# End of attention: an earlier division for the last group, rows scaled and written behind both halves' scores, one queue for the first half's scores

## The chip, the cores and the metric

The kernel runs on one core of one Trainium2 chip. The metric is the device time of the program in microseconds (us): the median of its runs. Engines are named as the profile names them: PE (matrix products and transposes), DVE (vector), ACT (activation), POOL (general), SP (issues transfers only).

## The reference, cut to what matters

The input `x` has 8 batches of 1024 tokens with 256 features. One layer of attention with 16 heads of 16 features, then a layer in which each of 8 experts picks the 1024 tokens that score highest for it:

```python
x = x + attention(layernorm(x), Wq, Wkv, Wout, bout)
xf = layernorm(x).reshape(-1, 256)              # 8192 rows
scores = softmax(xf @ gate_w.T, axis=-1)        # 8 experts
vals, idx = top_k(scores.T, 1024)               # each expert takes 1024 rows
y = layernorm(xf[idx]) * ln_w + ln_b
out = gelu(y @ fc1s + b1s) @ fc2s + b2s
xf = xf.at[idx].add(out * vals)                 # scattered back
x = x + xf
```

No expert can start before the scores of all 8192 tokens are known, since its threshold is found over all of them.

## The kernel before, in words

**Attention in steps.** The work is cut into 32 groups (8 batches, 4 groups of 4 heads each), and a group into 16 steps: two halves of 512 queries, 8 blocks of 128 keys in each. The loop counts steps `s` over all groups, from -13 to 512. In a step `step_pair` (twice) issues the score products (L581) and their exponentials on ACT (L614), and for a later group, 13 steps ahead, the products and maxima of L530 and L537. In every even step `weigh_values` multiplies the exponentials of the two steps before with the values (16 passes, L633), copies the result from PSUM with ACT (L642, L646) and adds it up on POOL (L648); the last sum of the last group's second half goes to DVE. At step 512 only the last `weigh_values` is left.

**Tasks between the steps.** What isn't part of that pattern is written as generators. `Task.advance` runs a generator up to its next `yield`: a number means "not for so many steps", a letter says what kind of piece comes next. `run_pieces` is called at the end of each step and advances each task in `urgent` once, and the first one in `ends`. When the last keys of a half were weighed, `weigh_values` puts `divide` (L652) in `urgent`. It waits 4 steps, becomes a piece of kind "y", and in the following step transposes the sums (L659), inverts the denominators (L665) and scales (L667). Once the last group of a batch has a half divided, the half's `epilogue` (L699) enters `ends`. Its pieces are, in order: nothing; the transposes of the attention output (L251, called from `transposed`) and their copies (L712); the output product of two token blocks and the residual sum (L719, L727); the same for the other two blocks; the statistics of one block (L219, L220), four times, the last followed by the scale (POOL, L222 and L224), the normalised rows `xf` (L242), the second layer norm's scale `rs_c` (POOL, L232 to L236), the sum `x + xf` (POOL, L733) and, in the last batch, the write of `out` (L734); transposes of `xf` (L251, L761); the gate product and its copy `lg` (L767, L775); transposition, maximum, difference and exponential (L778 to L786); the softmax's division into `sc` (L789 to L793); the transposition of the scores (L798), their copy `turned` (L800), four transfers of them into `by_expert` (L803), and in the last batch the scaled rows (L744, four, from `xf` and `rs_c` into `rows`) and their write to memory (L808).

**After the loop** `finish(urgent)` drives what is left of the divisions to the end at once, and the two epilogues of the last batch are advanced in turn, first half, second half, first half and so on, with no regard to the waits. When step 512 is over, the first half's epilogue has done its pieces up to the first output product, and the second half's hasn't begun.

**Order and buffers.** Each engine runs its instructions in the order of the text; a wait on one holds up all behind it on that engine. Inside attention this order is kept as written; the experts' part has a block of its own. `lg` and `turned` of both halves share one buffer (`tag="lg"`, `bufs=1`). In the last batch the first half's four transfers into `by_expert` are shared out between SP and ACT (L803: `last and t % 2`), as are the second half's.

**Search and experts.** DVE finds the threshold of all experts at once in 30 rounds over `by_expert` (L1003, with PE's L1007, then L1009 and L1012), makes the token lists, and POOL gathers rows from `rows_d` (L1146). The first weights are loaded by SP (L953, L955) behind the transfers of attention.

Of the kernel before, what the change touches and what calls it, by code (L numbers as in the profile page):

```python
# [19 lines left out]
P = 128  # L20
# [7 lines left out]
def preln_attention_moe_kernel(  # L28
# [18 lines left out]
    nc = tc.nc  # L47
    B, N, D = x.shape
    E = gate_t.shape[1]
    FF = fc1_t.shape[2]  # L50
    T = N // P
# [6 lines left out]
    NG = H // 4  # L58
# [5 lines left out]
    rows_d = dram.tile([B * N, ROW], F32, name="rows_d")  # L64
# [33 lines left out]
    with ExitStack() as actx:  # L98
# [10 lines left out]
        T2 = T // 2  # L109
# [514 lines left out]
        def weigh_values(i, half, chunk):  # L624

            b, g = divmod(i, NG)
            pa = ps_m.tile([P, QW], F32, tag="m", name="ps_av")
            for n, (kt, es) in enumerate(chunk):  # L630
                for h in range(4):
                    c = VS * (4 * g + h)
                    nc.tensor.matmul(  # L633
                        pa[HS * h : HS * (h + 1), :],
                        lhsT=v_bufs[b % 2][:, kt, c : c + HS],
                        rhs=es[h // 2][:, h % 2, :],
                        start=(n == 0),
                        stop=(n == len(chunk) - 1),
                    )
            if chunk[0][0] == 0:  # L640
                grp[i]["av"] = small.tile([P, QW], F32, tag="av", name="av")
                nc.scalar.copy(grp[i]["av"], pa)  # L642
            else:
                av = grp[i]["av"]
                part = small.tile([P, QW], F32, tag="avp", name="avp", bufs=3)
                nc.scalar.copy(part, pa)  # L646
                end = i == B * NG - 1 and half == 1 and chunk[-1][0] == T - 1
                (nc.vector if end else nc.gpsimd).tensor_tensor(av, av, part, ALU.add)  # L648
                if chunk[-1][0] == T - 1:
                    urgent.append(Task(divide(i, half, av)))  # L650

        def divide(i, half, av):  # L652

            b, g = divmod(i, NG)
            yield 4
            yield "y"
            pt = ps_m.tile([P, T2, 4, HS], F32, tag="m", name="ps_d")
            for t in range(T2):
                nc.tensor.transpose(  # L659
                    pt[:, t].rearrange("p h d -> p (h d)"), av[:, t * P : (t + 1) * P], ident  # L660
                )
            if b not in outs:
                outs[b] = side.tile([P, T, D], F32, tag="ao", name=f"ao_{b}")
            rden = small.tile([P, T2, 4, 1], F32, tag="rden", name="rden")
            nc.vector.reciprocal(rden, pt[:, :, :, DH : DH + 1])  # L665
            dst = outs[b][:, T2 * half : T2 * (half + 1), 4 * g * DH : 4 * (g + 1) * DH]
            nc.vector.tensor_tensor(  # L667
                dst.rearrange("p t (h d) -> p t h d", h=4),
                pt[:, :, :, 0:DH],
                rden.to_broadcast([P, T2, 4, DH]),  # L670
                ALU.mult,
            )
            finished[(i, half)] = True
# [17 lines left out]
        def add_bias(xt):  # L691
            nc.gpsimd.tensor_tensor(xt, xt, bo.unsqueeze(1).to_broadcast([P, T2, D]), ALU.add)

        def residual_ahead(b, hf):
            xt = residual(b, hf)
            yield 5
            add_bias(xt)

        def epilogue(b, hf):  # L699
            ao = outs[b]  # L700
            tok = slice(hf * QW, (hf + 1) * QW)
            last = b == B - 1
# [5 lines left out]
            own = last and hf == 1  # L708
# [4 lines left out]
            for t2 in range(T2 // 2):  # L713
                yield "x"
                po = ps_m.tile([P, 2, D], F32, tag="m", name="ps_o")
                for j in range(2):
                    t = 2 * t2 + j
# [16 lines left out]
            out_dma = lambda: nc.sync.dma_start(  # L734
                out[b, tok, :].rearrange("(t p) d -> p t d", p=P), xt
            )
            if last:
                out_dma()

            rows = side.tile([P, T2, ROW], F32, tag="rows", name=f"rows_{b}_{hf}")  # L740

            def rows_scaled():
                for t in range(T2):
                    eng.tensor_scalar(  # L744
                        rows[:, t, 0:D], xf[:, t, :], rstd2[:, t : t + 1], None, ALU.mult
                    )
# [53 lines left out]
            nc.scalar.copy(turned, ps[0 : T2 * E, 0:P])  # L800
            t0 = b * T + hf * T2
            for t in range(T2):
                (nc.scalar if last and t % 2 else nc.sync).dma_start(  # L803
                    by_expert[t0 // T2 :: NB, t * P : (t + 1) * P], turned[t * E : (t + 1) * E, :]
                )
            if last:
                rows_scaled()
            nc.sync.dma_start(  # L808
                rows_d[t0 * P : (t0 + T2) * P, :].rearrange("(t p) d -> p t d", p=P), rows
            )  # L810

# [56 lines left out]
        for s in range(-LEAD, n_steps + 1):  # L870
            i, step = divmod(s, 2 * T)
            b, g = divmod(i, NG)
            half, kt = divmod(step, T)
# [17 lines left out]
            if with_exp or with_max:  # L891
                es = []
                for pair in range(2):
                    es.append(
                        step_pair(
                            pair,
                            (mi, mstep) if with_max else None,
                            (i, half, kt) if with_exp else None,
                        )
                    )  # L900
                if with_exp:
                    if s % 2 == 0 and before:
                        weigh_values(*before[0][:2], [c[2] for c in before])
                        before = []
                    before.append((i, half, (kt, es)))
            elif before:
                weigh_values(*before[0][:2], [c[2] for c in before])
# [13 lines left out]
            for hf in range(2):  # L921

                if s >= 0 and b < B and finished.pop((NG * b + NG - 1, hf), None):
                    ends.append(Task(epilogue(b, hf), batch=b))
                if b > 0 and finished.pop((NG * b - 1, hf), None):
                    ends.append(Task(epilogue(b - 1, hf), batch=b - 1))
        finish(urgent)
        for hf in range(2):
            if finished.pop((NG * B - 1, hf), None):
                ends.append(Task(epilogue(B - 1, hf)))  # L930
# [488 lines left out]
```

## Time and profile before

| what | value |
|---|---|
| three runs | 2234.91, 2235.82, 2239.15 us; median 2235.82 |
| profiled execution | 2235.39 us, of which the span of instructions is 2233.4 |
| mean granted clock of PE | 0.968 |
| last exponential of attention (L614) ends | 1665.95 us |
| last 16 passes of L633 | 1665.01 to 1667.05 us |
| first half's `xf` (L242), second half's | 1678.79 us, 1686.22 us |
| first half's `turned`, second half's (L800) | 1691.26 us, 1696.34 us |
| first round of the search (L1003) | 1699.83 us |
| first gather (L1146) | 1761.31 us |

All times in the table and in what follows count from the first instruction of the span. The profile was taken of one execution; its page gives busy time by engine, 40 slices of the span, the chain of work that ended last, and groups of like instructions. The timeline lists single instructions with what ended the idle time ahead of them ("[2.17 <-DMA by_expert<-turned]"). The view of stretches gives, for each stretch from A to B, its length, the busy time of PE, PE's weight loads, DVE, ACT and POOL with the number of instructions, then PE's granted clock, the DMA engines' busy share and GB/s.

### The profile page before, as it was taken

The page shows a single profiled execution, that of the slowest core. Times are in us where ns is not written, and L with a number is a line of the kernel's source. Part 1 is how long each engine was busy: PE and PEld are TensorE (multiplying, and loading weights), DVE is VectorE, ACT ScalarE, POOL GpSimd, SP SyncE. Part 2 cuts the span into 40 slices and gives each one's busy share as a digit, 9 for nine tenths or more (in the row PEclk, how much of TensorE's full clock was granted, in tenths as well). Part 3 has the DMA queues.
Part 4 walks back from the last instruction along what each step waited for, and adds up shares of the span by engine and source line. Part 5 has one row for each costly group of instructions (what it writes and reads, how often), then busy time and mean ns, then how long its engine had stood idle before and what let it go on. Part 6 is the DMA issues. An engine that isn't in the chain of part 4 may idle for free.

```text
span 2233.4 us, 35022 instructions
## 1 busy us (share of the span) xinstructions
PE 2065.1 (92%) x12476; PEld 1098.2 (49%) x12476; DVE 1816.9 (81%) x3444; ACT 1382.3 (62%) x1782; POOL 1294.7 (58%) x1319
## 2 busy tenths in 40 slices
PE   7999899999999999999999999999982499999998
PEld 4444444444444444444444444444441266666665
DVE  7988788988898899889989988989936657777754
ACT  2677777877787877878778877877770012222222
POOL 6657666748585856758584766734142154555542
PEclk7999999999999999999999999999995699999999
DMA  6413723632362256236324722652113033333322
GB/s 182 168 59 129 268 75 130 228 135 78 134 238 87 89 205 212 90 111 234 130 77 154 269 73 79 218 174 85 41 39 134 20 74 72 76 76 75 70 48 25
DMA packets 152702, 271.51 MB, mean 122 GB/s; under 512 B 15056, under 2 KB 67664, under 8 KB 152400
## 3 DMA queue, kind: packets, MB, share of 16 engines
q1 hardware_dynamic: 139056, 250.61, 32.7%
q0 software_dynamic: 12288, 17.05, 4.6%
q8 instruction: 98, 1.61, 0.3%
q10 hardware_dynamic: 1184, 1.62, 0.2%
q14 instruction: 76, 0.62, 0.1%
HBM read 143.93 MB, written 125.04 MB: 120 GB/s over the span
## 4 chain that ended last, share of the span: by engine, by line
PE 70%; DVE 19%; issue 5%; DMA 2%; ACT 2%; POOL 1%; SPq 0%; POOLq 0%; ACTq 0%; DVEq 0%
PE ps_av L633 21%; DVE mx L537 14%; PE ps_x L530 13%; PE ps L1224 8%; PE ps_o L1278 7%; PE ps_s L581 7%; PE ps_p L288 6%; PE ps_t L251 3%; PE ps_o L719 3%; PE ps_h L1183 1%; ACT e L614 1%; DVE low L1123 1%; PE ps_d L659 1%; DMA top_d<-mrows 1%; DVE xr L727 1%
## 5 line engine op out<-in xcount | busy, mean ns | idle before, releaser
L537 DVE TENSOR_REDUCE mx<-ps_x 128x1 f32<-128x512 f32 x2048 | 1265.3, 682 | 162.5 <-PE ps_x L530 149.4
L614 ACT ACTIVATE e<-ps_s 128x1024 f32<-128x1024 f32 x1024 | 995.7, 1025 | 89.2 <-PE ps_x L530 39.9
L530 PE MATMUL ps_x<-k,q 64*128 64x512 f32 x2048 | 720.8, 452 | 19.7 <-DVE mx L537 7.0
L581 PE MATMUL ps_s<-q,s 64*128 64x512 f32 x2048 | 624.3, 429 | 9.2 <-ACT e L614 6.0
L530 PEld LDWEIGHTS ps_x<-k,q 64*128 64x128 f32 x2048 | 348.5, 186 | 416.5 <-DVE mx L537 286.3
L633 PE MATMUL ps_av<-e,v 128*32 128x512 f32 x4096 | 495.9, 602 | 7.4 <-DVE mx L537 1.3
L648 POOL TENSOR_TENSOR av<-av,avp 128x512 f32<-128x512 f32 x191 | 243.7, 1276 | 404.7 <-ACT avp L646 383.4
L581 PEld LDWEIGHTS ps_s<-q,s 64*128 64x128 f32 x2048 | 314.6, 185 | 47.8 <-ACT e L614 30.3
L1288 POOL DMA_INDIRECT out<-o,idx x64 | 114.9, 1796 | 216.1 <-DVE o L1287 80.5
L1278 PE MATMUL ps_o<-w,hT 128*128 128x256 f32 x1024 | 230.2, 381 | 0.0
L633 PEld LDWEIGHTS ps_av<-e,v 128*32 128x32 f32 x4096 | 107.6, 109 | 244.5 <-issue 165.8
L1278 PEld LDWEIGHTS ps_o<-w,hT 128*128 128x128 f32 x1024 | 191.8, 190 | 29.3 <-issue 4.8
L646 ACT COPY avp<-ps_av 128x512 f32<-128x512 f32 x192 | 112.7, 587 | 148.5 <-PE ps_av L633 145.9
L1236 ACT COPY mid<-ps 128x512 f32<-128x512 f32 x28 | 16.0, 571 | 203.7 <-PE ps L1224 203.7
L288 PE MATMUL ps_p<-wqkv,xnT 128*128 128x512 f32 (+1 forms) x288 | 134.5, 596 | 6.0 <-DVE mx L537 5.3
L1176 ACT ACTIVATE hT<-mid,b 128x512 f32<-128x512 f32 x112 | 77.9, 718 | 98.9 <-DVE mid L1251 73.9
L269 POOL TENSOR_TENSOR u<-pe,sin 128x256 f32<-128x256 f32 (+1 forms) x128 | 86.2, 696 | 56.5 <-ACT pe L263 56.5
L1146 POOL DMA_INDIRECT g<-rows_d,idx x64 | 70.0, 1094 | 83.5 <-issue 75.2
L1286 DVE TENSOR_TENSOR o<-ps_o,b2b 128x256 f32<-128x256 f32 x64 | 27.0, 422 | 103.2 <-PE ps_o L1278 93.7
L335 POOL CAST hi<-full 128x512 fp32r<-128x512 f32 x60 | 36.8, 614 | 90.3 <-ACT full L333 83.7
L273 POOL TENSOR_TENSOR qk<-pe,u 128x512 f32<-128x512 f32 (+1 forms) x72 | 83.3, 1157 | 7.6 <-DVE pe L271 2.6
L336 POOL TENSOR_TENSOR lo<-full,hi 128x512 fp32r<-128x512 f32 x60 | 77.0, 1283 | 6.7 <-DMA s_d<-dlo 2.1
(194 smaller groups left out, 2368.9 us busy)
## 6 DMA issues: line engine op xcount, KB each, us to landing
s<-s_d SPq DMA_DIRECT2D x64, 512.0 KB
k<-k_d SPq DMA_DIRECT2D x62, 512.0 KB
q<-q_d SPq DMA_DIRECT2D x124, 256.0 KB
s_d<-dhi SPq DMA_DIRECT2D x32, 512.0 KB
s_d<-dlo SPq DMA_DIRECT2D x32, 512.0 KB
w<-in_fc_t SPq DMA_DIRECT2D x16, 1024.0 KB
q_d<-hi SPq DMA_DIRECT2D x30, 512.0 KB
q_d<-lo SPq DMA_DIRECT2D x30, 512.0 KB
```

Source lines behind the costliest of these rows:

```text
L269: eng.tensor_tensor(u[:, :, a * hd : (a + 1) * hd], v4[:, :, 1 - a, :], s3, ALU.mult)
L288: nc.tensor.matmul(pp, lhsT=xnT[:, kc, t % T2 * P : (t % T2 + 1) * P], rhs=w.rearrange("p a d -> p (a d)") if n == DC else w, start=(kc == 0),
L530: nc.tensor.matmul(pt, lhsT=q[r : r + 64, h // 2, j * P : (j + 1) * P], rhs=k[r : r + 64, h // 2, kh * QW : (kh + 1) * QW], start=True, st ...
L537: nc.vector.tensor_reduce(grp[i]["mx"][:, kh, h, j : j + 1], pt, AX.X, ALU.max)
L581: nc.tensor.matmul(pt[:, h % 2, :], lhsT=ones_r[r : r + 64, :] if last else k[r : r + 64, pair, kt * P : (kt + 1) * P], rhs=(top_bufs[half ...
L614: nc.scalar.activation(e.rearrange("p h q -> p (h q)"), pt.rearrange("p h q -> p (h q)"), AF.Exp, scale=DH**-0.5,)
L633: nc.tensor.matmul(pa[HS * h : HS * (h + 1), :], lhsT=v_bufs[b % 2][:, kt, c : c + HS], rhs=es[h // 2][:, h % 2, :], start=(n == 0), stop= ...
L646: nc.scalar.copy(part, pa)
L648: (nc.vector if end else nc.gpsimd).tensor_tensor(av, av, part, ALU.add)
L1224: nc.tensor.matmul(ph, lhsT=lhsT, rhs=rhs, start=True, stop=True)
L1278: nc.tensor.matmul(po, lhsT=h[:, f, j * P : (j + 1) * P], rhs=weights[e][1][:, f, :], start=(n == 0), stop=(n == FC - 1),)
L1288: nc.gpsimd.indirect_dma_start(out=out_rows[:, :], out_offset=bass.IndirectOffsetOnAxis(ap=idx[:, t : t + 1], axis=0), in_=o, in_offset=No ...
```

## The change

Five things change, all of them at the end of attention. In `weigh_values` the last sum of both halves of the last group goes to DVE. `divide` waits two steps for the last group and four for all others. In the last batch's epilogues `out` isn't written behind its sum any more, the rows aren't scaled and written by each half for itself, and both are put on the list `left`; the second half, once its scores are on their way, scales both halves' rows, then writes the rows and `out` of each. The first half's four transfers of scores all go to SP (`own` is true for the last batch's second half alone).

```diff
-                end = i == B * NG - 1 and half == 1 and chunk[-1][0] == T - 1
+                end = i == B * NG - 1 and chunk[-1][0] == T - 1
                 (nc.vector if end else nc.gpsimd).tensor_tensor(av, av, part, ALU.add)
...
         def divide(i, half, av):
 
             b, g = divmod(i, NG)
-            yield 4
+            yield 2 if i == B * NG - 1 else 4
             yield "y"
...
+        left = []
 
         def epilogue(b, hf):
...
-            if last:
-                out_dma()
...
-                (nc.scalar if last and t % 2 else nc.sync).dma_start(
+                (nc.scalar if own and t % 2 else nc.sync).dma_start(
                     by_expert[t0 // T2 :: NB, t * P : (t + 1) * P], turned[t * E : (t + 1) * E, :]
                 )
+            rows_out = rows_d[t0 * P : (t0 + T2) * P, :].rearrange("(t p) d -> p t d", p=P)
             if last:
-                rows_scaled()
-            nc.sync.dma_start(
-                rows_d[t0 * P : (t0 + T2) * P, :].rearrange("(t p) d -> p t d", p=P), rows
-            )
+
+                left.append((rows_scaled, rows_out, rows, out_dma))
+                if hf == 1:
+                    for scale, *_ in left:
+                        scale()
+                    for _, rows_out, rows, write in left:
+                        nc.sync.dma_start(rows_out, rows)
+                        write()
+            else:
+                nc.sync.dma_start(rows_out, rows)
```

## The prediction

> **What bounds the kernel now.** I read the page's busy shares and slices first, then the chain of waits, then the timeline of all engines between attention and the experts.
>
> ```profile
> PE 2065.1 (92%) x12476; PEld 1098.2 (49%) x12476; DVE 1816.9 (81%) x3444; ACT 1382.3 (62%) x1782; POOL 1294.7 (58%) x1319
> PEclk7999999999999999999999999999995699999999
> ```
>
> TensorE carries the kernel, except in slices 30 and 31 (1675 to 1787 us), where its clock is halved: there one chain runs from attention's last sums to the search for the experts' thresholds (30 rounds of 1.40 us from 1699.83), and nothing else is left to do. The diff touches only the 45 us ahead of that search, and the search needs both halves' scores. So the sum is one question: when does DVE's first L1003 start? From there to the first expert's gather (1761.31) each instruction waits for the one before it, so an earlier start moves the end by as much. The chain of waits on the way:
>
> ```profile
> 1683.78 0.20 DVE lm L781
> 1683.98 0.02 issue
> 1684.00 0.19 DVE z L783
> 1684.20 0.34 DVE bnst L219
> ...
> 1691.26 0.27 ACT turned L800
> 1691.53 0.02 issue
> 1691.55 1.42 ACTq L803
> 1692.96 0.03 issue
> 1692.99 3.21 DMA by_expert<-turned
> ...
> 1696.34 0.27 ACT turned L800
> 1696.61 0.02 issue
> 1696.63 0.58 SPq L803
> 1697.20 0.05 issue
> 1697.25 2.54 DMA by_expert<-turned
> 1699.80 0.03 issue
> 1699.83 0.77 DVE ge L1003 x2
> ```
>
> The reader sees the second half held up by the first three times. (1) Its last statistics (L219, 1684.11) stand behind the first half's logits on DVE, though DVE had been free since 1681.78. (2) Its exponential is ready at 1691.70, but ACT first issues two of the first half's score transfers (1.42 + 0.65 us) and runs it at 1693.69: 2.0 us. (3) Its `turned` is one buffer with the first half's: the scores were transposed at 1695.10, the copy waits until 1696.34 for the first half's transfers to land: 1.2 us.
>
> **The change, part by part.** Times are from the span's start. I replay the stage with the rows' durations, each engine in its order.
>
> *Division after two steps.* Only the first half feels it (the second half's division is driven to its end after the loop anyway). Every piece moves two steps forward: division from step 509 to 507, transposes (L251) from 511 to 509, the two output products (L719) from 512 and behind it to 510 and 511, the first statistics into 512.
> - Division: 0.66 us of PE where it idles 0.97 (ahead of 1655.17): free.
> - Transposes: 1.09 us of PE where the division was and 0.43 more was idle: free. Their two copies take two ACT slots of 0.47, so step 510's exponentials run 0.94 later and end their slot at 1663.62; the next copy waited for PE until 1663.52 anyway: 0.1.
> - First product: 8 passes, a slot of 1.83 (1666.99 to 1668.82). It now stands ahead of step 511's scores: 1663.33 to 1665.16. Scores 0.66, then the second product to 1667.65, then the last 16 passes of L633.
>
> ```profile
> 1665.01 2.04 PE L633 MATMUL ps_av<-e,v 128*32 128x512 f32 x16
> 1666.99 1.99 PE L719 MATMUL ps_o<-wo,aoT 128*128 128x256 f32 x8
> ```
>
> These passes end at 1669.58 instead of 1667.05: **2.5 us lost.** Before, both products lay in gaps of the second half's chain. With the products gone from there the chain gets some back: copy, sum (1671.07), division (to 1672.49, was 1670.33), transposes at 1672.6 (was 1670.98, behind the second product), products from 1673.88 (was 1672.26): 1.6 late.
> - First half on DVE: three statistics of 0.55 from 1672.46, POOL 0.23 + 1.04, scaling from 1675.67 (was 1678.79): 3.1 early. Its transposes hold PE from 1676.23 to 1677.68, ahead of the second half's second product (1677.68 to 1679.78, was over at 1676.03). Logits: gate product to 1680.25, copy 0.27, transposition 0.28, maximum at 1681.0 (was 1683.78). The gate product at full clock is not in the trace: between 0 and the 1.40 seen at half clock; I take 0.7.
> - The second half's four statistics, in between: 1680.43, 1681.33, 1682.42, 1682.97; the last ends at 1683.60 (was 1684.75): **1.15 won**, hold-up (1) all but gone.
> - From there rows repeat: POOL, scaling at 1685.07, 4.21 us to the logits' copy (1686.22 to 1690.43), so 1689.28.
>
> *DVE instead of POOL for the sum at step 504:* 0.69 for 1.28, needed only at step 507: nothing.
>
> *First half's scores on SP alone.* ACT issues none of them, so hold-up (2) goes: **2.0 won.** SP issues four of about 0.6 from 1683.17 to 1685.58; they land, as the last ones did (1697.84 to 1699.80), 2.0 later, 1687.5. They now come ahead of the second half's `lg`, which shares the buffer and wants it at 1689.28: 1.7 spare. Late next would be that copy, by whatever the landing exceeds.
>
> *Hold-up (3)* goes with it: `turned` has only its own transposition ahead of it: **1.2 won.** It runs at 1692.02, and with 3.2 from the first issue to the search (1696.63 to 1699.83) the search starts at 1695.5. How long a transfer takes with less beside it is between 1.39 (the small write of L565 at 1635.76) and 3.21 from its issue; I keep the 2.54 of the last one.
>
> *Rows scaled and written behind.* Eight L744 in slots of 0.265: 2.1 us of DVE, 1691.5 to 1693.6, while the scores fly until 1695.5: hidden, 1.9 spare. One of them took 2.44 us beside POOL's L733 (2.45); L733 would now be over at 1689.5; without that cover 2.4 us are due, 0.5 behind the spare. On SP four issues (0.38 to 0.64) follow the scores; behind them wait the first weights (wanted at 1769), and nothing reads rows before 1761 or adds to `out` before 1790: hidden by 60 us.
>
> **Sum:** 1.15 + 1.97 + 1.2 = 4.3 us. The profiled execution took 2235.39 (span 2233.4 and 2.0 around it), so 2231.1; the median of the runs stands 0.43 above it, so **2231.5**.
>
> **Rivals.**
> *The clock halves early.* The replay leaves PE 1.0 us of work in the 3.4 us from 1669.6 to 1673.0. The trace has such a gap:
>
> ```profile
> 447.34:450.75 3.41, 1.39 (x8) 0.77 (x9) 2.43 (x6) 1.52 (x3) 3.14 (x5) 1.00 0.22 85
> 450.75:454.17 3.42, 3.42 (x19) 1.28 (x21) 2.95 (x8) 2.05 (x2) 3.42 (x4) 0.50 0.91 258
> ```
>
> PE was busy for 1.39 of 3.41, and the next 3.4 us ran at 0.50; a stretch with 1.54 (225.49) kept 1.00. Then the second half's two products take 1.8 more each, partly beside waits, and the last statistic comes at about 1687.6: the search starts near 1699.5, if the halving lasts; if it is over after 3.4 us, near 1697. Time 2233 to 2235.5. It depends on where such a stretch begins: with starts from about 1668.7 to 1670.2 of 3.4 the work is below 1.4. For it: that share, 44%; against: one row alone halves at so much work, and a shorter halving still leaves most of the gain. I put it at 26%. [...]
>
> *Two weights ahead of the second half's scores.* SP issued the first weight (L953, 1693.35) ahead of the second half's scores (1696.63), so the order on SP isn't the text's. With the first two (2.1 MB) going from 1689, at 257 to 375 GB/s, the scores land up to 2 us later: 2233.5. 6%.
>
> *All four ahead (the slower side).* SP is free from 1685.6 to 1692; if all four weights (4.2 MB) are issued there, at the slowest 257 GB/s seen they run until 1705.3, and the scores on SP land behind them: 5.5 us later than now, 2241. It decides from the third weight on (2.8 MB by 1699.8). Against: the other weights were issued only behind the last rows' write (1698.63 and later). 6%.
>
> *It doesn't do what it says:* the first half's logits still stand in the way of the last statistic; only (2) and (3) go, 2232.6. 4%.
>
> **How the numbers follow.** Forecast 58%, with 3 to 6.3 us won: 0.6 more with a quicker landing, 1.25 more with the second half's transposes and gate product at full clock, 1.4 less if the products cost more ahead of the scores. About two thirds of it lie beyond 4.5 us, 0.2% of the time, which is what a measurement of this kernel tells from no change. Faster by over 0.2%: 0.39 from these and 0.01 of the rest, 0.40; slower, from the four weights, 0.06; within 0.2%, the rest, 0.54. The range reaches from 2228.8 (6.3 won and 0.3 of spread) to 2236.5 (the early halving with the 1 us by which the runs differ) and leaves out the slower side.
>
> **What would show it.** L633's last 16 passes end near 1669.6, with two L719 ahead of them; the first half's L242 near 1675.7; the second half's last L219 near 1683; L786 directly behind L783; `turned` with no wait for a DMA; all L744 between the scores' issue and L1003; L1003 first at about 1695.5. It is wrong if the clock is 0.50 ahead of 1679, if SP has weights ahead of the scores that land late, or if PE's last scores slip by more than 2.5.

## The result and the profile after

| | before | after |
|---|---|---|
| median of 20 runs each | 2235.90 us (2231.35 to 2239.98) | 2232.12 us (2227.76 to 2237.15) |
| ratio, 95% interval | | 0.9982 (0.9975 to 0.9990) |
| profiled execution, its span | 2235.39, 2233.4 us | 2233.80, 2231.7 us |

The change wins 4.0 us (2.2 to 5.6), 0.18% of the time; 2231.5 us had been forecast. Executions of one kernel differ by some 9 us, more than the change is worth, so the place of the gain is read from the traces.

The page of the changed kernel shows nothing of it. These are its lines of busy time and of the granted clock; the clock's digits are those of before, and no engine's busy time moved by more than 3.5 us:

```profile
PE 2065.7 (93%) x12476; PEld 1099.3 (49%) x12476; DVE 1817.3 (81%) x3445; ACT 1381.8 (62%) x1782; POOL 1291.2 (58%) x1318
PEclk7999999999999999999999999999995699999999
```

One thing must be taken out before the traces are laid side by side. Near 1650 us, ahead of all that was changed, the view of stretches of the changed kernel shows the clock halved once (columns: length, busy time of PE, PE's weight loads, DVE, ACT, POOL with counts, granted clock, DMA share, GB/s):

```profile
1647.30:1650.72 3.42, 2.19 (x17) 0.76 (x9) 1.48 (x1) 2.80 (x5) 2.24 (x1) 1.00 0.00 0
1650.72:1654.13 3.41, 3.41 (x18) 0.59 (x16) 0.00 (x0) 1.57 (x2) 0.00 (x0) 0.50 0.07 19
```

The execution profiled of before has no such stretch. Ahead of it the changed kernel's execution was 0.78 us early (score products of L581 at 1650.40 for 1651.18 in before), behind it 0.86 late (1654.32 for 1653.46). So the halving cost 1.64 us, and this stage starts 0.87 us later. That is why the times below are distances from one instruction that both kernels have and that lies ahead of the change: the 16 passes of L633 at step 510 (1661.47 in before, 1662.34 after). **D** is the distance from there to the first round of the search. It is 38.36 in before and 35.63 after; from the search to the first gather each takes 61.5.

| distance from the passes of step 510, us | before | forecast | after |
|---|---|---|---|
| last 16 passes of L633 end | 5.58 | 8.11 | 8.29 |
| first half's `xf` (L242) | 17.32 | 14.20 | 14.34 |
| first half's maximum (L781) | 22.31 | 19.53 | 19.60 |
| second half's last statistic ends | 23.28 | 22.13 | 22.15 |
| second half's `xf` | 24.75 | 23.60 | 23.63 |
| second half's `lg` (L775) | 28.96 | 27.81 | 27.83 |
| second half's exponential (L786) | 32.22 | 29.10 | 29.11 |
| second half's `turned` (L800) | 34.87 | 30.55 | 30.61 |
| its first score issue (L803) | 35.16 | 30.83 | 30.89 |
| first round of the search (D) | 38.36 | 34.03 | 35.63 |

The lines that answer to those shown of before (some numbers are shifted: L721 is the old L719, L735 and L736 the old L733 and L734, L814 the old L808, L1010 the old L1003). In the timeline the first half's first output product runs from 1664.19, step 511's scores from 1666.12, and the second product stands directly ahead of the last passes of L633:

```profile
1666.78 1.99 PE L721 MATMUL ps_o<-wo,aoT 128*128 128x256 f32 x8
...
1668.70 1.92 PE L633 MATMUL ps_av<-e,v 128*32 128x512 f32 x16
```

And the chain of waits:

```profile
1691.23 0.20 DVE z L783
1691.45 0.24 ACT z L786
...
1692.95 0.26 ACT turned L800
1693.23 1.42 ACTq L803
1694.66 0.03 issue
1694.68 2.98 DMA by_expert<-turned
```

The exponential stands right behind the difference, and `turned` behind it by the softmax and a transposition alone: the waits for ACT's issues and for the first half's landing are gone. But the 1.42 us of ACT's first issue, which the first half's scores took before, is now on the second half's path, and from that issue to the search (1697.97) it takes 4.74 us; the forecast had put 3.2 there. The timeline of the two queues at that place:

```profile
1693.23 1.20 SPq L803 DMA_DIRECT2D by_expert<-turned  x2
1693.23 2.06 ACTq L803 DMA_DIRECT2D by_expert<-turned  x2
1694.53 0.40 SPq L814 DMA_DIRECT2D rows_d<-rows  x1
1694.98 0.50 SPq L736 DMA_DIRECT2D out<-xr  x1
```

### The profile page after: what moved, and what is told of

The parts are those of the page before. It is cut to its first block, busy times and chain, and to the rows that moved or that the text cites. A ratio compares the mean times of both kernels' runs of the same rounds, so it can differ in the third digit from the quotient of the medians.

```text
span 2231.7 us, 35022 instructions
## 1 busy us (share of the span) xinstructions
PE 2065.7 (93%) x12476; PEld 1099.3 (49%) x12476; DVE 1817.3 (81%) x3445; ACT 1381.8 (62%) x1782; POOL 1291.2 (58%) x1318
## 4 chain that ended last, share of the span: by engine, by line
PE 68%; DVE 19%; issue 5%; POOL 3%; DMA 3%; ACT 2%; SPq 0%; POOLq 0%; ACTq 0%; DVEq 0%
PE ps_av L633 20%; DVE mx L537 13%; PE ps_x L530 13%; PE ps L1231 8%; PE ps_o L1285 7%; PE ps_s L581 7%; PE ps_p L288 6%; PE ps_t L251 3%; PE ps_o L721 2%; PE ps_h L1190 1%; POOL xf L242 1%; ACT e L614 1%; DVE low L1130 1%; PE ps_d L659 1%; DMA top_d<-mrows 1%
## 5 line engine op out<-in xcount | busy, mean ns | idle before, releaser
L581 PE MATMUL ps_s<-q,s 64*128 64x512 f32 x2048 | 625.3, 429 | 8.0 <-ACT e L614 5.0
L633 PE MATMUL ps_av<-e,v 128*32 128x512 f32 x4096 | 494.9, 601 | 7.4 <-DVE mx L537 1.3
L581 PEld LDWEIGHTS ps_s<-q,s 64*128 64x128 f32 x2048 | 315.2, 186 | 46.5 <-ACT e L614 27.0
L633 PEld LDWEIGHTS ps_av<-e,v 128*32 128x32 f32 x4096 | 107.5, 109 | 243.9 <-issue 163.9
```

Of the source, the lines that this page charges most:

```text
L581: nc.tensor.matmul(pt[:, h % 2, :], lhsT=ones_r[r : r + 64, :] if last else k[r : r + 64, pair, kt * P : (kt + 1) * P], rhs=(top_bufs[half ...
L633: nc.tensor.matmul(pa[HS * h : HS * (h + 1), :], lhsT=v_bufs[b % 2][:, kt, c : c + HS], rhs=es[h // 2][:, h % 2, :], start=(n == 0), stop= ...
```

## The experiments

All of them compute the whole layer. Each was run in five rounds against the kernel before. The differences sought (1 to 6 us) are within the spread of single runs, so each experiment is judged by D of its profiled execution and by the lines of its trace; the ratio stands beside it. How far D of one execution can be trusted shows in the changed kernel run twice.

**The changed kernel again.**

> The changed kernel unchanged, for a second profile of the stage: the runs of the change and of before differ by 4.0 us (2.2 to 5.6), the distances of the two profiles by 2.7. Theory (the distance is set by the order of the instructions, and the rest of a run's spread lies ahead of the stage): distance 35.3 to 35.9 again. Rival (the landing of the scores varies by more than 1 us from run to run): another distance, 34 to 35 or over 36.

D is 35.66, 0.03 from the first; median 2232.12 us against 2235.95, ratio 0.9989 (0.9977 to 1.0001). In the fourteen profiles the passes of step 510 start anywhere from 1657.2 to 1665.1 us: most of what runs differ by lies ahead of this stage.

### Does one part carry the gain?

**The early division alone** (before, with the last sum on DVE and two steps for four).

```diff
-                end = i == B * NG - 1 and half == 1 and chunk[-1][0] == T - 1
+                end = i == B * NG - 1 and chunk[-1][0] == T - 1
...
-            yield 4
+            yield 2 if i == B * NG - 1 else 4
```

> The kernel before with the earlier division (and its sum on DVE) alone. Read as the distance from the 16 passes of L633 at step 510 to the first round of the search: 38.4 us before, 35.6 with the whole change. Theory (the parts only work together): the second half's write of out now stands on SP ahead of two of the first half's score transfers, and waits for POOL's last sum; so these transfers land near 1692 to 1693 on the scale of before, the second half's logits, which share their buffer, wait 3 to 4 us for them, and little or nothing is won: 37 to 38.4, time within 1.5 us of before. Rival (the division is the gain): 34 to 35, some 4 us faster than before.

D 37.40; 2235.47 us against 2235.04, ratio 0.9999 (0.9990 to 1.0009). Its timeline, at the second half's `lg`:

```profile
1680.12 10.01 SPq L734 DMA_DIRECT2D out<-xr  x2
...
1693.17 0.27 ACT L775 COPY lg<-ps_g 128x128 f32<-128x128 f32 x1 [4.69 <-DMA by_expert<-turned]
```

The two writes of `out` hold SP from 1680.12 to 1690.13: the second one waits there for the second half's sum on POOL, over at 1689.73. The first half's scores have been ready since 1683.3, but SP's two of them wait behind that write and go at 1690.23; `lg`, which shares their buffer, waits for their landing and comes 3.87 later than in the changed kernel (31.70 for 27.83). So only 0.96 of D is won: the rest is lost in a queue that the division does not touch.

**The first half's scores on SP alone** (before, with the change's condition in L803).

```diff
-                (nc.scalar if last and t % 2 else nc.sync).dma_start(
+                (nc.scalar if own and t % 2 else nc.sync).dma_start(
```

> The kernel before with the first half's scores on SP alone, and nothing else. Theory: the exponential of the second half runs 2.0 us earlier, but its scores' copy still waits for the first half's transfers, which now end later (four issues of 0.6 on one queue): distance 38 to 39.5, no gain. Rival (the 2.0 us that ACT spends on issuing are won by themselves): 36.4, 2 us faster.

D 40.91, later than before by 2.55 and beyond what was expected; 2236.22 us, ratio 1.0001 (0.9990 to 1.0012). The exponential comes 2.0 earlier, as it should. Timeline:

```profile
1697.89 0.45 SPq L953 DMA_DIRECT2D w<-in_fc_t  x1
...
1698.59 0.25 ACT L800 COPY turned<-ps_sc 32x128 f32<-32x128 f32 x1 [3.31 <-DMA by_expert<-turned]
```

The first weight (1 MB) is issued ahead of the second half's scores; rows and the second weight are issued while ACT still issues its late pair (1698.87 to 1700.93, the first of them 1.42); the search starts 4.8 us after the last score issue, where it took 2.0 in before.

**Rows and `out` behind the scores, alone** (the changed kernel with the old division and both queues).

```diff
-                end = i == B * NG - 1 and chunk[-1][0] == T - 1
+                end = i == B * NG - 1 and half == 1 and chunk[-1][0] == T - 1
...
-            yield 2 if i == B * NG - 1 else 4
+            yield 4
...
-                (nc.scalar if own and t % 2 else nc.sync).dma_start(
+                (nc.scalar if last and t % 2 else nc.sync).dma_start(
```

> The kernel before with rows and out scaled and written behind both halves' scores, and nothing else. Theory: the first half's scores have less beside them and land up to 0.8 us sooner, the copy of the second half's scores waits less: distance 37.6 to 38.4. Rival (the writes that stood in front were the cost): 36 or less, 2 us or more faster.

Missed: D 39.69; 2236.99 us, ratio 1.0006 (0.9997 to 1.0015). With nothing of its own to write, SP issues two weights (at 28.48 and 30.87), one ahead of the first half's scores and one between the halves; those scores land late, and `turned` waits 4.70 us for them.

**The change without the early division.**

```diff
-                end = i == B * NG - 1 and chunk[-1][0] == T - 1
+                end = i == B * NG - 1 and half == 1 and chunk[-1][0] == T - 1
...
-            yield 2 if i == B * NG - 1 else 4
+            yield 4
```

> The change without the earlier division (its sum on POOL again for the first half): queue and rows alone. Theory: the first half's scores come when the second half's logits are already out (copy at 29.3), four issues on SP, both weights go ahead of or between the scores, and the second half's wait for them: distance 39.5 to 41.5, 1 to 3 us slower than before. Rival (two of the three parts are enough): 36 or less.

D 39.91; 2236.27 us against 2235.95, ratio 1.0008 (0.9996 to 1.0020). Again two weights are issued early, at 28.49 ahead of the first half's scores and at 32.08 ahead of the second half's, and `turned` waits 4.47 us for the first half's landing.

**The change with rows and `out` ahead, as before.**

```diff
             if last:
-                left.append((rows_scaled, rows_out, rows, out_dma))
...
+                rows_scaled()
```

(and `out_dma()` behind its sum again).

> The change without its third part: rows and out are scaled and written by each half for itself again, with the earlier division and the first half's scores on SP. Theory: all four of the first half's score transfers now stand on SP behind the second half's write of out, which waits for POOL's sum (28.3), so the shared buffer is free only at about 33 and the second half's logits wait for it: distance 39 to 41, 1 to 3 us slower than before. Rival (the rows' place costs nothing): 35.6.

D 40.74; 2238.93 us, ratio 1.0013 (0.9999 to 1.0027). All four score issues of the first half stand behind the held write of `out`, from 28.77 on; `lg` comes at 32.62.

So no part alone gains more than 1.0 in D, and neither pair that has the queue in it gains at all; the three together gain 2.7. The division brings the first half's scores forward, the moved writes free SP for them, and scores that go early are ahead of the weights. The third pair, division and rows without the queue, comes next.

### What the missing 1.5 us is

**The change with both queues for the first half's scores** undoes the third part only.

```diff
-                (nc.scalar if own and t % 2 else nc.sync).dma_start(
+                (nc.scalar if last and t % 2 else nc.sync).dma_start(
```

> The changed kernel, but the first half's scores go to SP and ACT in turn, as before. In the changed kernel ACT's first score transfer took 1.42 us to issue and its second 0.65, in the kernel before the same held of the first half's, and the second half's took 0.57 each. Theory (ACT's first transfer after a long pause is slow to issue, whichever half it is): the second half's take 0.57 each, distance 34.8 or a little less, 0.8 us or more faster than the change. Rival (it is slow because SP issues beside it): unchanged, 35.6.

D 33.73, 1.9 better than the change; 2231.69 us against 2235.04, ratio 0.9981 (0.9970 to 0.9992). The timed runs can't tell it from the change (0.9982 and 0.9989); the traces can. Its chain of waits:

```profile
1695.98 0.58 SPq L803
...
1696.61 1.90 DMA by_expert<-turned
```

The first half's pair takes the 1.42 us now, at 21.87, where nothing waits for it: the second half's `lg` still comes at 27.78. The second half's issues are 0.58 each on both queues, done 1.2 after the first began, ahead of the first write of rows (1697.28), and the search starts 1.7 after that (1698.87). So once the division is early, putting the first half's scores on one queue loses time.

**ACT woken.** The change as it is, with a 4 KB transfer that nobody waits for, issued by ACT some 19 us ahead of its scores.

```diff
+            if own:
+                woken = dram.tile([8, P], F32, name="woken")
+                nc.scalar.dma_start(woken, x[0, 0:8, 0:P])
             for t2 in range(T2 // 2):
```

> The change, with one small transfer (4 KB from memory to memory) issued by ACT behind the second half's copies of L714, some 17 us ahead of ACT's first score transfer. Theory (the first transfer after a long pause is slow to issue, and the late issue then stands behind the rows' writes): the score transfers take 0.57 to 0.65 each to issue, distance 33.7 to 34.2 as in e4, against 35.6 in the change. Rival (it is slow for another reason, or the pause of 17 us is already long enough): 1.42 and 35.6.

D 34.12; 2232.97 us, ratio 0.9981 (0.9970 to 0.9992). The idle transfer takes 1.25 us to issue, and ACT's two scores then 1.44 together instead of 2.06. That alone gives back 1.5 of the 1.9. Its timeline:

```profile
1673.36 1.25 ACTq L717 DMA_DIRECT2D woken<-in_x  x1
...
1692.19 1.44 ACTq L806 DMA_DIRECT2D by_expert<-turned  x2
```

So the price is one of ACT's first issue, not of these transfers. ACT had issued nothing since it loaded Wq and Wkv at 0.8 and 1.3 us.

**Weights behind the scores.** Not the change, but the kernel of the second experiment, with POOL copying one element per partition from `by_expert` into the first expert's weight tiles, so that their loads wait for the scores.

```diff
+        if e == 0:
+            nc.gpsimd.tensor_copy(w1[:, 0, 0:1], by_expert[:, QW - 1 : QW])
         nc.sync.dma_start(w1, fc1_t[e].rearrange("(c p) f -> p c f", p=P))
```

(and the same for `w2`)

> e2 (the kernel before with the first half's scores on SP alone), but the first expert's two weights are loaded only when all scores have landed (POOL writes one element per partition of them from by_expert first). In e2 the second half's scores landed 4.8 us after their last issue, with both weights and a rows' write issued ahead of it: distance 40.9. Theory (2 MB of weights ahead on the same DMA engines): landing 2 to 2.4 us after the last issue at 36.1, distance 38.0 to 38.5, near the kernel before. Rival (the landing was slow for another reason): 40 to 41.

D 38.27 instead of 40.91; 2236.46 us, ratio 0.9997 (0.9986 to 1.0008). With the two weights ahead of the scores, that kernel's search comes 2.6 us later.

### What the 2.5 us on PE cost

**Products held.** The kernel with both queues, its two first-half products put behind the last 16 passes of L633.

```diff
-                yield "x"
+                yield (n_steps,) if last and hf == 0 and t2 == 0 else "x"
...
+        for _ in range(2):
+            ends[0].advance(n_steps)
         while ends:
```

> e4 (the change, with the first half's scores on both queues), but the first half's two output products are held until the last values are weighed, so that PE's last scores and last 16 passes don't stand behind them; the first half keeps its place in the order behind them. Distance as before (step 510's passes to the search): 33.7 in e4. Theory: the last passes end 2.5 to 3 us earlier, but the first half's second product then falls behind the division of the second half and its statistics start at 9.8 instead of 9.65, so only what the second half's products gain is left: 0.9 us, distance 32.8. Rival (the 2.5 us on PE were lost one for one): 31.2 or less.

Neither: D 33.72 (33.73 with the products ahead); 2232.14 us against 2236.12, ratio 0.9979 (0.9967 to 0.9990). The last passes end at 5.76 instead of 8.29, and nothing comes of it. The first half's first statistic waits for the products instead, at 10.50 (9.65 in the change), its `xf` comes at 14.19 (14.34), and the second half follows that. The first half's chain and the second half's wait for the same PE, and to put one ahead delays the other: the second half's last statistic ends at 22.0 (22.15 in the change), although its sums were ready 2.5 earlier.

### A version written from these results

**The order written out.** The last pieces of both halves in an order by hand, so that the second half's statistics stand ahead of the first half's `xf`; products held; the second scale, the sums `x + xf` and the rows on POOL behind all scores; the first half's `turned` in a buffer of its own; ACT woken.

```diff
-            turned = small.tile([T2 * E, P], F32, tag="lg", name="turned", bufs=1)
+            turned = small.tile([T2 * E, P], F32, tag="tail" if last and hf == 0 else "lg", name="turned", bufs=1)
...
-        for _ in range(2):
-            ends[0].advance(n_steps)
+        for n, times in ((0, 4), (1, 3), (0, 1), (1, 3), (0, 1), (1, 2), (0, 3), (1, 1), (0, 2), (1, 1), (0, 1)):
+            for _ in range(times):
+                ends[n].advance(n_steps)
```

> The change with the last pieces' order written out: products held as in e5, the second half's products ahead of the first half's transposes on PE, the second half's four statistics ahead of the first half's logits on DVE, the sums, scales and rows of both halves on POOL behind all scores, the first half's turned scores in a buffer of their own, and one small transfer by ACT some 14 us ahead of its first score transfer. Theory (what is left is the order of the two halves on PE and DVE, and ACT's slow first issue): statistics done at about 18 instead of 22, distance 28.5 to 30, some 4 to 5 us less than e4 and 8 to 10 less than before. Rival (the first half's chain is the bound, as e5 would show): 32 to 33.

Missed: D 33.46, though `turned` is ready at 28.04; 2231.53 us, ratio 0.9981 (0.9970 to 0.9992). And from the search to the gather it takes 63.4 instead of 61.5. The weight is one cause: it is issued at 1685.41, 0.9 ahead of the last scores, whose issues end at 1687.8, and the search starts 3.7 later. The timeline shows the other:

```profile
1696.94 0.16 DVE L1033 SCALAR_TENSOR_TENSOR cand<-drop,cand 128x1 int32<-128x1 int32 x1
1697.01 4.64 POOL L756 TENSOR_TENSOR xr<-xr,xf 128x1024 f32<-128x1024 f32 x2
...
1698.34 1.03 DVE L1033 SCALAR_TENSOR_TENSOR cand<-drop,cand 128x1 int32<-128x1 int32 x1
```

Beside POOL's two sums of 2.3 us each, a step of the search that takes 0.16 us takes 1.03, and 1.06 in the next round, each time until that sum is over.

**The same with the weights behind the scores,** rows and the second half's sum on DVE, the first half's sum on POOL ahead of the search.

```diff
+        if e == 0:
+            nc.gpsimd.tensor_copy(w1[:, 0, 0:1], by_expert[:, QW - 1 : QW])
...
-                    nc.gpsimd.tensor_scalar(
+                    eng.tensor_scalar(
...
+                    nc.vector.tensor_tensor(xt, xt, xf, ALU.add)
```

> e6 with two repairs: the first expert's weights are loaded only when all scores have landed (in e6 one was issued 0.9 us ahead of the second half's scores, which landed 3.7 us after their last issue), and the rows are scaled on DVE again (on POOL they slowed the search's rounds by 1.9 us in all). Theory: the scores land 1.7 to 2.0 us after their last issue at 29.8, distance 31.4 to 31.9, and 61.5 from the search to the first gather; 6 to 7 us less than before. Rival (the landing is slow whatever stands ahead): 33.5.

D 31.77, and 61.51 from there to the gather; 2229.01 us against 2235.95, ratio 0.9972 (0.9961 to 0.9984), 6.3 us less than before. The lowest median and D of all kernels here. Its chain of waits, with nothing large ahead of the scores:

```profile
1685.77 0.62 ACTq L813
...
1686.43 2.12 DMA by_expert<-turned
```

The search starts at 1688.97, 3.2 us after the first score issue: the forecast's 3.2, with ACT woken and nothing ahead.

## Why the prediction was right, and which term was off

**The replay** of the order held: nine marks between the last passes of L633 and the second half's first score issue lie within 0.2 us of the forecast, seven of them within 0.1.

**Hold-up (1), 1.15 us:** measured 1.13 (last statistic at 22.15 for 23.28).

**Hold-up (2), 1.97 us:** 1.98 (the exponential gains 3.11 in all, 1.13 of it from the first).

**Hold-up (3), 1.2 us:** 1.15 (`turned` gains 4.26 in all).

**The transfer is the mis-sized term.** The forecast kept the "3.2 from the first issue to the search" of before. It took 4.74, and 1.5 of the 4.3 us went. Of these, 0.86 is issuing: ACT's pair took 2.06 us, where before the second half's pair on each queue was done in 1.2. The row with 1.42 stands among the lines of the prediction, in the chain of waits, and was read as belonging to the first half's transfers. It belongs to ACT's first issue since the loads at the kernel's start, and a change that takes the first half's issues off ACT moves it to the second half. The other 0.7 is the landing: SP now has the first write of rows at 1694.53 and `out` at 1694.98, ahead of the end of ACT's last issue (1695.29). The packets in the trace show which of the two it was: those of the rows (528 KB) move from 1695.46 to 1697.14, those of ACT's last transfer only from 1697.00 to 1697.17, and those of `out` come behind. ACT's last 4 KB are through 1.88 us after their issue ended; with ACT woken, where no packet of rows goes ahead of them, it is 0.99. With both queues for the first half, or with ACT woken, both shares go (D 33.73 and 34.12, against the forecast's 34.03). So the forecast's D was right for a kernel that issues its last scores as fast as before.

**The 2.5 us lost on PE** are there (8.29 for 5.58, 2.7 us). They were rightly not subtracted: taken away in the kernel with both queues, D stays at 33.72.

**Rows hidden:** the eight L744 run in 2.18 us from 1692.26, none beside a POOL sum. They begin 0.97 ahead of the scores' issue, not behind it as the prediction's sign had it, but nothing on DVE waits for them, and they are over 3.5 us ahead of the search. Their cost is the 0.7 us just named: it was SP's write of them, which the prediction had "follow the scores", that met ACT's late pair.

**The early halving** (26%) came in neither profile of the change. In the first of them the clock changed next 30.72 us behind the end of the single halving near 1650 (1654.13 to 1684.85), nine stretches of 3.41. Counted on in such steps, the two stretches that bear on it are these:

```profile
1671.19:1674.61 3.42, 1.93 (x14) 1.55 (x14) 2.83 (x10) 0.87 (x3) 0.00 (x0) 1.00 0.00 0
...
1681.44:1684.85 3.41, 0.60 (x2) 0.24 (x2) 2.77 (x13) 0.56 (x3) 0.44 (x2) 1.00 0.00 0
```

PE was busy for 1.93 us in the first, and the clock stayed at 1.00. That doesn't refute the rival: its condition, a stretch there with less than 1.4, came up in neither profile. But its share of 44% was too high. Where the replay left PE 1.0 us of work in 3.4, it had 1.35 (1670.47 to 1673.88), and only stretches that begin within 0.37 us (1670.30 to 1670.67) have less than 1.4, which is 11% of 3.41. Both shares are estimates: they take it that a stretch can begin anywhere with the same chance, and that the clock halves behind less than 1.4, from the one row with 1.39. No run shows such a limit: the clock halved behind 2.19 of 3.42 us too (1650.72), and stayed at 1.00 behind these 1.93. Behind the second, with 0.60, the clock went to 0.50 (1684.85; in before at 1679.56). In the two kernels with the order written out it halved at 18.4 and 19.4 from the passes of step 510, earlier than in the change (22.5 and 23.0), and one of them is still the fastest kernel here: the halving isn't what decides in this stage. Whether some of the timed runs of the change had it early can't be told from their times.

**Weights ahead of the scores** were priced right in kind. In the change one weight did go ahead of the second half's scores (1690.16), and its 1 MB was through at 1694.75, ahead of the end of their last issue (1695.29). In the kernels with SP free too early, one or two went at a bad time, and the search came up to 2.6 us later; this did make D longer than before (39.7 to 40.9). The prediction had put that only from the third weight on; two were enough here. The change escapes it because its first half's scores are issued early (1684.20, 6 us ahead of that weight).

**The time:** the trace gives 2.73 us, and the timed runs 4.0 (2.2 to 5.6), which holds 2.73; the runs of the repeat give 2.5 (0.2 slower to 5.1 faster). That the forecast of 4.3 came out so near to the first timed value is luck: its sum was 1.6 us above what the traces give.

## What to carry to other kernels

Before work is moved behind a queue's end, list for each queue what it then issues first: a queue that is set free takes the next thing in its program (weights of 1 MB, at 28.48 and 30.87 with rows and `out` moved alone), and an issue that is slow once (ACT's first in this stage, 1.42 us) moves to where it hurts when the transfers that paid it go to another queue. Read a long row (1.42 beside 0.57) as a price of its place in time until its neighbours show otherwise, and see where that place will be after the change. Parts of a change that gain little or lose alone can gain much together when each removes the wait that the other runs into: in D the early division alone won 0.96, the moved writes alone lost 1.33, and the two together won 4.63. The whole is then also run without each part: here the third one, a single queue for the first half's scores, cost 1.9 of that.

## What the runs showed of the hardware

**ACT's first issue since the kernel's start.** Some 1670 to 1700 us after the loads of Wq and Wkv it took 1.41 to 1.43 us where SP issued at the same time, and 1.17 and 1.25 where SP didn't; the issues behind it took 0.57 to 0.78. A transfer 18 to 19 us earlier still helped (0.62 and 0.78). After pauses of 7 and 11 us (from the end of one issue to the next), where both queues serve both halves, the price was not paid again: 0.57 each. SP didn't pay it after pauses of 29 to 33 us (0.37 to 0.58 an issue), nor after one of 113 us (0.37). So not every queue pays after every pause; whether ACT's price is one of a pause between 18 and 1670 us or of its first issue in this part of the program stays open. To issue from both queues saved 0.35 us here: four issues on SP took 2.41 us, two each on SP and this ACT 2.06. It did not keep their transfers apart: in the change ACT's last 4 KB (1697.00 to 1697.17) went behind SP's rows (from 1695.46).

**Small transfers behind large ones.** The scores (4 KB a transfer) were taken up by the search 1.4 to 2.0 us after their last issue where no write of rows was issued among them or its packets came behind theirs. It was 2.6 to 3.1 where the first rows (528 KB) went ahead of ACT's last 4 KB (the change and four other kernels or profiles), and 3.7 and 4.8 where a weight (1 MB) was issued 0.9 to 1.0 us ahead of the first score. A weight issued 3.0 us ahead, as in the kernel with both queues, still left it at 1.7.

**A POOL sum beside DVE.** In the kernel with the order written out, DVE's step over two tensors of one column went from 0.16 to 1.06 us, to the end of POOL's sum; the comparison over 512 columns, with a single tensor and one value per partition, kept 0.75. What sets the two apart no run shows.

**The clock.** The single halving near 1650 us lasted 3.41 us and cost 1.64; four of the fourteen profiles have one there (the others at 1648.4, 1650.3 and 1658.6). The same program had it in one execution and not in another: in the changed kernel's two profiles the 16 passes of L633 at that place took 3.51 us (from 1650.88) and 1.92 (from 1650.56). PE's busy time in the 3.4 us ahead does not tell it: the clock halved behind 2.19 of 3.42 us here and behind 2.07 of 3.41 in the fastest kernel (1676.57), and stayed behind 1.93 of 3.42 in the change (1671.19) and behind 2.19 of 3.41 in before (1648.84). What decides it no run shows.
